# The scales of layer 2's norm, and its transposes, given out one step later than the statistics they need

## Chip, cores and metric

One core of a Trainium2 chip runs the whole program. The metric is the time on the device, in microseconds. The kernel before took 2642.23 us (median of three runs, 2640.15 to 2648.64); its profiled execution has a span of 2645.6 us.

## What is computed

Sixteen graphs of 1024 nodes with 256 features each go through four layers of graph network. Each layer normalises its input, applies relu, and adds its result to the stream `x`:

```python
h = jnp.maximum(_layernorm(x, axis=-1), 0.0)
x = x + _L2_gnn_ref(h, adj, L2_gnn_W_msg, L2_gnn_W_upd, L2_gnn_bias)
```

Layers 0, 1 and 3 are attention over the adjacency matrix (layer 3 with four heads and a norm of its own). Layer 2, whose norm the change is about, has no attention: it averages over the neighbours.

```python
h = jnp.einsum('bnf,fu->bnu', x, W_msg)
msg_sum = jnp.einsum('bij,biu->bju', a, h)
deg = jnp.sum(a, axis=1)
messages = jnp.where(deg[..., None] > 0, msg_sum / jnp.maximum(deg, 1.0)[..., None], 0.0)
out = jnp.einsum('bnf,fu->bnu', x, W_upd) + messages + bias
return jax.nn.relu(out)
```

## The kernel before

**Tiles.** A graph's stream `xs` lies in SBUF as eight tiles of 128 nodes x 256 features. Each layer has three steps: the norm with a transposition of its result into `ht` (features on partitions); a projection of the eight tiles (`project`, L678); and the product with the attention weights or the adjacency matrix (L749, L805, L868 and L874, L930). At the end of the products of layers 0 to 2, for i = 0 to 7, `residual` (from L719) adds the result to tile i of `xs`, and the statistics for the next layer's norm are taken there.

**The norm.** The class `Norm` works on pairs of tiles, g = 0 to 3. `pair` gets the sums of two tiles from `residual`, makes `shift`, the negative mean, on VectorE (L638), and lets ScalarE square the shifted tiles and sum them (L643, output `unread`). After every second pair, `stds` calls `inv_std`: GpSimd scales the four variances (L592) and raises them to the power -1/2 (L593), which gives `rs`. For layers 0, 1 and 3 the transposed values are only shifted, `hn = relu(x - mean)`, and the factor `rs` is applied after the projection. So their `hn` doesn't wait for the power. `shifted` makes two `hn` on ScalarE (L659), and `flip` transposes the two `hn` that are waiting (four transposes on TensorE, L672) and copies the result to `ht` (L673). `flip` is called one step after `shifted`, when the next pair begins.

Layer 2 differs: its norm (built with `times`, the degrees of the nodes) multiplies by the standard factor and by the degree before the transposition. So it needs `rs` first. `stds` makes two products on VectorE (L621 and L622): `scales[0] = rs * degree`, `scales[1] = scales[0] * shifts`. Then both pairs, g - 1 and g, are given out on the spot: `shifted` for pair g - 1, `flip`, `shifted` for pair g. That happens twice in layer 1's product: at i = 3 for tiles 0 to 3 and at i = 7 for tiles 4 to 7.

**The order of the work.** Each layer is a generator, and `graph(b)` runs a graph's layers one after the other. Each `yield` gives a number, the time that the step is taken to last in units of its own; a loop at the end of `tile_simple_stack` always continues the generator whose time comes first, and starts a new graph every 120 units (`APART`). A graph lasts some 237 units, and a tail of its own (`tail`, L942 to L992) follows, so the end of layer 1 of one graph is traced between the end of layer 3 and the tail of the graph before it and the first norm and layer 0's projection of the graph after it. That gives the program order. From it a planner makes each engine's queue: among the instructions that it takes to be ready, by costs of its own, the one traced first goes next. So an instruction can be issued earlier than its place in the program when the engine would otherwise stand. `later(...)` pins an instruction behind everything already traced on its engine. The tail's last products on VectorE are pinned in this way (L979, L982, L984, L986, L990), and so are most DMAs on the SyncE queue.

**Buffers concerned.** `hn` has three buffers, the PSUM tiles of the transposes (`tr`) two, those of the projections (`mm`) two, `ht` two, `rs` six. They are shared by all graphs under way.

**Lines.** L589 to L673 are `inv_std` and `Norm`; L719 to L729 `residual`; L792 and L736 copy a projection out of PSUM in layers 1 and 0 (`hs`), L859 and L861 in layer 2 (`hi`, `rest`); L826 to L830 are the end of layer 1 (`shares`, `e`, `v`); L1002 to L1006 the loop over the layers.

Of the kernel before, what the change touches and what calls it, by code (L numbers as in the profile page):

```python
# [11 lines left out]
OP = mybir.AluOpType  # L12
# [409 lines left out]
def tile_simple_stack(  # L422
# [11 lines left out]
    nc = tc.nc  # L434
    B, N, D = x.shape
    NT = N // P
# [111 lines left out]
    class Mask:  # L548
# [4 lines left out]
        def __init__(self, b):  # L553
            self.b, self.next, self.raws = b, 0, []
            self.bytes = None
            for _ in range(self.AHEAD):
                self.load()
# [31 lines left out]
    def inv_std(var, n, scale, eps):  # L589

        rs = small.tile([P, NT * H], F32, tag="rstd", name="rs", bufs=6)
        nc.gpsimd.tensor_scalar(rs[:, :n], var, scale, eps, op0=OP.mult, op1=OP.add)  # L592
        nc.gpsimd.tensor_tensor(rs[:, :n], rs[:, :n], neg_half[:, :n], op=OP.pow)  # L593
        return rs

    def new_ht():
        return state.tile([P, DC, N], F32, tag="ht", name="ht", bufs=2)

    class Norm:
# [4 lines left out]


        def __init__(self, times=None):
            self.ht, self.rs, self.waiting, self.times = new_ht(), [], None, times
            if times is not None:
                self.shifts = small.tile([P, NT], F32, tag="shifts", name="shifts", bufs=2)
                self.scales = small.tile([P, 2, NT], F32, tag="scales", name="scales", bufs=2)  # L610
            self.mv = small.tile([P, NT, 2], F32, tag="mv", name="mv", bufs=4)
            self.mean, self.var = self.mv[:, :, 0], self.mv[:, :, 1]

        def stds(self, n, scale):

            k = len(self.rs)
            rs = inv_std(self.var[:, k : k + n], n, scale, 1e-5)
            self.rs += [rs[:, i : i + 1] for i in range(n)]
            if self.times is not None:
                part = slice(k, k + n)  # L620
                nc.vector.tensor_tensor(self.scales[:, 0, part], rs[:, :n], self.times[:, part], op=OP.mult)  # L621
                nc.vector.tensor_tensor(self.scales[:, 1, part], self.scales[:, 0, part], self.shifts[:, part], op=OP.mult)  # L622

        def pair(self, xs, g, sums=None):

            if self.times is None:
                self.flip()
                shift = small.tile([P, 2], F32, tag="shift", name="shift")
            else:
                shift = self.shifts[:, 2 * g : 2 * g + 2]  # L630
            if sums is None:
                for k in range(2 * g, 2 * g + 2):
                    st = small.tile([P, 6], F32, tag="bn", name="st")
                    nc.vector.bn_stats(st, xs[:, k, :])
                    nc.vector.bn_aggr(self.mv[:, k, :], st)
                nc.vector.tensor_scalar(shift, self.mean[:, 2 * g : 2 * g + 2], -1.0, None, op0=OP.mult)
            else:
                nc.vector.tensor_scalar(shift, sums, -1.0 / D, None, op0=OP.mult)  # L638
            if self.times is None:
                self.shifted(xs, g, [(1.0, shift[:, k : k + 1]) for k in range(2)])  # L640
            if sums is not None:
                for k in range(2):
                    nc.scalar.activation(  # L643
                        unread, xs[:, 2 * g + k, :], AF.Square, bias=shift[:, k : k + 1], accum_out=self.var[:, 2 * g + k : 2 * g + k + 1]
                    )
            if sums is None and g == NT // 2 - 1:
                self.stds(NT, 1.0)
            elif sums is not None and g % 2:
                self.stds(NT // 2, 1.0 / D)
                if self.times is not None:  # L650
                    for gg in (g - 1, g):
                        self.flip()
                        self.shifted(xs, gg, [[self.scales[:, k, n : n + 1] for k in range(2)] for n in (2 * gg, 2 * gg + 1)])

        def shifted(self, xs, g, by):
            hns = []
# [62 lines left out]
    def residual(xs, i, v, after, e=None):  # L719

        x = xs[:, i, :]
        if i % 2 == 0:
            after.flip()
            after.sums = small.tile([P, 2], F32, tag="sums", name="sums")
        if e is not None:
            nc.vector.scalar_tensor_tensor(x, e, 1.0, x, op0=OP.min, op1=OP.add)  # L726
        nc.vector.scalar_tensor_tensor(x, v, 0.0, x, op0=OP.max, op1=OP.add, accum_out=after.sums[:, i % 2 : i % 2 + 1])  # L727
        if i % 2:
            after.pair(xs, i // 2, after.sums)  # L729


    def layer0(b, xs, m, norm, after):
# [40 lines left out]
        for i in range(NT):  # L773
            if i < EARLY:
                ps = early[i]
            else:
                ps = at_ps.tile([P, HALF], F32, tag="at", name="ps_o0")
                for j in range(NT):
                    product(ps, i, j)
            e = work.tile([P, D], F32, tag="e", name="e")  # L780
            nc.scalar.activation(e, ps[:, :D], AF.Exp)  # L781
            v = work.tile([P, D], F32, tag="v", name="v")
            nc.scalar.copy(v, ps[:, :D])
            residual(xs, i, v, after, e)
            yield 3.9


    def layer1(b, xs, mask, norm, after):
# [28 lines left out]
        for i in range(NT):  # L817
            if i < EARLY:
                ps = early[i]
            else:  # L820
                ps = at_ps.tile([P, HALF], F32, tag="at", name="ps_o1")
                for j in range(NT):
                    product(ps, i, j)
            k = b * NT + i
            z = shares[:, k : k + 1]
            nc.vector.reciprocal(z, ps[:, D : D + 1])  # L826
            e = work.tile([P, D], F32, tag="e", name="e")
            nc.scalar.activation(e, ps[:, :D], AF.Exp, scale=z)
            v = work.tile([P, D], F32, tag="v", name="v")
            nc.scalar.activation(v, ps[:, :D], AF.Copy, scale=z)  # L830
            residual(xs, i, v, after, e)
            yield 3.74


    def degrees(b):

        t = small.tile([P, NT], F32, tag="deg", name="deg", bufs=2)
        halves = squares[:, b * NT * NHALF : (b + 1) * NT * NHALF].rearrange("p (n g) -> p n g", g=NHALF)
        nc.vector.tensor_tensor(t, halves[:, :, 0], halves[:, :, 1], op=OP.add)
        return t  # L840
# [48 lines left out]
    def layer3(b, xs, mask, norm, res):  # L889
# [5 lines left out]
        for n in range(NT):  # L895
            ps = project(norm, wx[3], n, W3)
            nc.scalar.activation(hs[:, n, :], ps[:, :W3], AF.Copy, scale=norm.rs[n])
            if n % 2:
                pair = slice(n - 1, n + 1)
                nc.scalar.activation(hbv[:, pair, :, HO], terms[:, pair, H:], AF.Exp, scale=S3)  # L900
                t = hbv[:, pair, :, :HO]
                hv = hs[:, pair, :D].rearrange("p t (h e) -> p t h e", e=HO)
                bias = rows["bias3"].rearrange("p (h e) -> p h e", e=HO).unsqueeze(1).to_broadcast([P, 2, H, HO])
                nc.vector.tensor_tensor(t, hv, bias, op=OP.add)
                nc.vector.tensor_tensor(t, t, hbv[:, pair, :, HO:].to_broadcast([P, 2, H, HO]), op=OP.mult)
            yield 1.15
# [87 lines left out]
    def graph(b):  # L994
        xs = loaded.pop(b)
        m = masks.pop(b)
        norm = Norm()
        for g in range(NT // 2):
            norm.pair(xs, g)
            m.step()  # L1000
            yield 2.66
        for layer, inputs in ((layer0, (m,)), (layer1, (m.bytes,)), (layer2, ())):  # L1002
            yield 2.36
            norm.flip()
            after = Norm(degrees(b) if layer is layer1 else None)
            yield from layer(b, xs, *inputs, norm, after)  # L1006
            norm = after
        yield 1.44
        norm.flip()
        res = state.tile([P, NT, H, HW], F32, tag="res", name="res", bufs=1)  # L1010
        hs = yield from layer3(b, xs, m.bytes, norm, res)
        return tail(b, xs, hs, res)
# [22 lines left out]
    weights01(0, w0, w0_t, a0, (0, 1), wait=False)  # L1035
    next(loads_0)
    queue = [(32, 0, more())] + [(b * APART, b, graph(b)) for b in range(B)] + [(b * APART - 80, b, loads(b)) for b in range(1, B)]
    while queue:
        queue.sort(key=lambda g: g[:2])
        at, b, g = queue.pop(0)  # L1040
# [86 lines left out]
```

## Time and profile before

| | of the span of 2645.6 us |
|---|---|
| TensorE matmuls | 2470.5 us, 93% |
| TensorE weight loads | 2096.2 us, 79% |
| VectorE | 1969.1 us, 74% |
| ScalarE | 1449.8 us, 55% |
| GpSimd | 378.7 us, 14% |
| `hn` with scales (L659) | 128 x 592 ns |
| `scales` (L621, L622) | 64 x 0.16 us |
| transposes (L672) | 1024 x 273 ns |
| power (L593), four elements a partition, POOL free | 1.01 us |

The profile names engines PE (TensorE matmul), PEld (weight load, which overlaps PE), DVE (VectorE), ACT (ScalarE), POOL (GpSimd). A line of its timeline gives the start in microseconds from the span's start, the length, the engine, the source line, the operation, what is written and read, the shape, and in brackets the idle time of the engine just before and what ended it. In the answers for a tile, "its engine sat idle before it" lists the idle time before instructions that touch the tile, and "who waited for it" the idle time of others, each in microseconds in total and number of times. In steady state the trace repeats itself with every graph, some 158 us apart.

### The profile page before, as it was taken

The numbers are of one execution on the slowest core, as the hardware profiler recorded it, in microseconds if no ns is written. First come the engines' busy times: TensorE is split into PE (matmuls) and PEld (weight loads), VectorE is DVE, ScalarE is ACT, GpSimd is POOL, SyncE is SP. The second block draws the span as 40 slices with busy tenths as digits, with TensorE's granted clock in tenths as the row PEclk, the third lists the DMA queues.
The fourth block names the chain that finished last, engine by engine and source line by source line (L and its number), as shares of the span: only waits on it lengthen the run. The fifth ranks groups of instructions, "written<-read, shape, count | busy, mean of one in ns | idle before, by whom it ended". The sixth has DMA issues, their size and how long they took to land.

```text
span 2645.6 us, 62817 instructions
## 1 busy us (share of the span) xinstructions
PE 2470.5 (93%) x26194; PEld 2096.2 (79%) x26194; DVE 1969.1 (74%) x3813; ACT 1449.8 (55%) x4065; POOL 378.7 (14%) x390
## 2 busy tenths in 40 slices
PE   5899999999999999999999999999999999999985
PEld 4688787887878878787887878878787887878864
DVE  4357777787777877778787777877778787777858
ACT  4564755637555374654737556374754737556350
POOL 1010111102111020111102111020111102111011
PEclk7899999999999999999999999999999999999997
DMA  4431241414215142241414215141241414214021
GB/s 152 115 81 57 91 111 58 124 58 129 72 54 152 58 117 70 66 135 57 124 54 132 69 57 152 61 123 60 81 121 58 124 54 132 69 57 124 26 64 35
DMA packets 146073, 233.75 MB, mean 88 GB/s; under 512 B 9393, under 2 KB 94513, under 8 KB 145777
## 3 DMA queue, kind: packets, MB, share of 16 engines
q1 hardware_dynamic: 74608, 145.73, 17.3%
q0 software_dynamic: 71168, 83.89, 13.0%
q8 instruction: 208, 3.41, 0.5%
q14 instruction: 89, 0.72, 0.1%
HBM read 212.35 MB, written 17.24 MB: 87 GB/s over the span
## 4 chain that ended last, share of the span: by engine, by line
PE 60%; DMA 14%; ACT 10%; DVE 9%; issue 5%; POOL 2%; SPq 0%; DVEq 0%; ACTq 0%; POOLq 0%
PE ps_o L749 14%; PE ps_proj L678 14%; PE ps_o L930 10%; PE ps_o L805 8%; PE ps_o L874 6%; DMA raw<-in_adj_t 5%; PE pt_h L672 4%; DMA adj<-in_adj 4%; DVE p L920 3%; PE ps_o L868 3%; DMA row<-d_row 2%; ACT mask L575 2%; ACT hs L810 2%; ACT unread L643 2%; ACT hn L659 1%
## 5 line engine op out<-in xcount | busy, mean ns | idle before, releaser
L920 DVE SCALAR_TENSOR_TENSOR p<-row,q,mask 128x1024 f32<-128x1024 f32 x512 | 633.5, 1279 | 66.1 <-PE ps_o L930 53.2
L930 PEld LDWEIGHTS ps_o<-hb,p 128*64 128x64 f32 x16384 | 503.9, 138 | 99.9 <-issue 47.5
L930 PE MATMUL ps_o<-hb,p 128*64 128x65 f32 x16384 | 543.1, 224 | 19.8 <-ACT res L938 10.3
L805 PE MATMUL ps_o<-hs,p 128*128 128x257 f32 x2048 | 510.7, 392 | 31.0 <-DVE p L812 17.2
L678 PE MATMUL ps_proj<-wx,ht 128*128 128x258 f32 (+2 forms) x2048 | 515.7, 390 | 3.3 <-ACT hs L736 1.1
L749 PE MATMUL ps_o<-hs,p 128*128 128x256 f32 x2048 | 492.2, 385 | 13.6 <-ACT hs L763 13.3
L805 PEld LDWEIGHTS ps_o<-hs,p 128*128 128x128 f32 x2048 | 370.1, 191 | 96.1 <-ACT v L830 24.5
L749 PEld LDWEIGHTS ps_o<-hs,p 128*128 128x128 f32 x2048 | 380.7, 192 | 65.0 <-ACT hs L763 16.5
L678 PEld LDWEIGHTS ps_proj<-wx,ht 128*128 128x128 f32 x2048 | 361.9, 190 | 80.4 <-ACT rest L861 11.6
L726 DVE SCALAR_TENSOR_TENSOR xs<-e,xs 128x256 f32<-128x256 f32 x256 | 108.4, 424 | 261.0 <-ACT e L781 168.9
L592 POOL TENSOR_SCALAR rs<-mv 128x4 f32<-128x4 f32 (+1 forms) x112 | 44.3, 395 | 1583.2 <-ACT unread L643 1568.0
L659 ACT ACTIVATE hn<-xs,shift 128x256 f32<-128x256 f32 x384 | 177.1, 502 | 126.9 <-DVE shift L638 126.6
L593 POOL TENSOR_TENSOR rs<-rs,neg_half 128x4 f32<-128x4 f32 (+2 forms) x144 | 242.8, 1689 | 10.7
L672 PE MATMUL pt_h<-ident,hn 128*128 128x128 f32 x1024 | 181.1, 284 | 41.8 <-ACT hn L659 40.5
L874 PE MATMUL ps_o<-hi,adj 128*128 128x258 f32 x1024 | 202.9, 322 | 15.9 <-DMA adj<-in_adj 14.7
L938 ACT ACTIVATE res<-ps_o 128x260 f32<-128x260 f32 x128 | 44.4, 380 | 310.9 <-PE ps_o L930 310.9
L575 ACT ACTIVATE mask<-raw 128x512 uint8<-128x512 int32 x256 | 160.2, 627 | 76.5 <-DMA raw<-in_adj_t 75.8
L672 PEld LDWEIGHTS pt_h<-ident,hn 128*128 128x128 f32 x1024 | 121.3, 141 | 102.0 <-ACT hn L659 78.2
L874 PEld LDWEIGHTS ps_o<-hi,adj 128*128 128x128 f32 x1024 | 151.6, 190 | 33.3 <-DMA adj<-in_adj 20.3
L727 DVE SCALAR_TENSOR_TENSOR xs<-v,xs 128x256 f32<-128x256 f32 x384 | 161.2, 423 | 19.6 <-ACT v L830 1.0
L759 DVE SCALAR_TENSOR_TENSOR p<-row,q 128x1024 f32<-128x1024 f32 x128 | 160.2, 1272 | 20.2 <-DMA row<-d_row 20.2
L874 PE MATMUL ps_o<-lo,adj 128*128 128x258 f32 x1024 | 163.7, 293 | 0.0
(108 smaller groups left out, 2902.5 us busy)
## 6 DMA issues: line engine op xcount, KB each, us to landing
raw<-in_adj_t SPq DMA_DIRECT2D x256, 256.0 KB
adj<-in_adj POOLq DMA_DIRECT2D x64, 1024.0 KB, 6.0
row<-d_row SPq DMA_DIRECT2D x112, 512.0 KB
xs<-in_x POOLq DMA_DIRECT2D x32, 512.0 KB, 5.5
out<-xs SPq DMA_DIRECT2D x32, 512.0 KB
wx<-in_w SPq DMA_DIRECT2D x3, 256.0 KB
d_row<-e_row SPq DMA_DIRECT2D x48, 4.0 KB
wts<-in_w_t SPq DMA_DIRECT2D x2, 256.0 KB
```

What stands on the lines that cost most here:

```text
L575: nc.scalar.activation(self.bytes[:, n, g * HALF : (g + 1) * HALF], raw, AF.Square, accum_out=squares[:, k : k + 1])
L593: nc.gpsimd.tensor_tensor(rs[:, :n], rs[:, :n], neg_half[:, :n], op=OP.pow)
L659: nc.scalar.activation(hn, xs[:, 2 * g + k, :], AF.Relu, scale=scale, bias=bias)
L672: nc.tensor.transpose(pt[:, c, k * P : (k + 1) * P], hn[:, c * P : (c + 1) * P], ident)
L678: nc.tensor.matmul(ps[:, :width], norm.ht[:, c, n * P : (n + 1) * P], w[:, c, :width], start=(c == 0), stop=(c == DC - 1))
L727: nc.vector.scalar_tensor_tensor(x, v, 0.0, x, op0=OP.max, op1=OP.add, accum_out=after.sums[:, i % 2 : i % 2 + 1])
L749: m = nc.tensor.matmul(ps[:, :D], ps_[j][:, i * P : (i + 1) * P], hs[:, j, :D], start=(j == 0), stop=(j == NT - 1))
L759: nc.vector.scalar_tensor_tensor(p, row_a, q[:, j : j + 1], row_b, op0=OP.mult, op1=OP.max)
L805: nc.tensor.matmul(ps[:, : D + 1], ps_[j][:, i * P : (i + 1) * P], hs[:, j, : D + 1], start=(j == 0), stop=(j == NT - 1))
L874: nc.tensor.matmul(ps[:, : D + 2], adj_n[g][:, i, jj : jj + P], h[:, i, : D + 2], start=False, stop=(h is lo and i == NT - 1), skip_group_ ...
L920: nc.vector.scalar_tensor_tensor(p, row, q[:, jj, h : h + 1], mask[:, jj, :], op0=OP.max, op1=OP.mult)
L930: nc.tensor.matmul(pss[g][part, k * HW : (k + 1) * HW], ps_[t][:, i * P : (i + 1) * P][:, part], hbv[:, j + t, h, :], start=(j == 0 and t ...
```

## The change

The statistics stay where they are. `pair` notes after every second pair that a part of layer 2's norm is due, and the scales, the relu and the transposes of that part are given out by a new function, `settle`. It is called by `residual` before every odd tile, so for tiles 0 to 3 at i = 5 rather than at i = 3, and before the next layer begins, so for tiles 4 to 7 after layer 1's last step, two yields (3.74 and 2.36 units) later in the program. It is meant to keep the engines' queues from standing before instructions whose statistics are still under way. For the other norms `due` is None and `settle` does nothing. The arithmetic is the same.

```diff
@@ class Norm
         def __init__(self, times=None):
-            self.ht, self.rs, self.waiting, self.times = new_ht(), [], None, times
+            self.ht, self.rs, self.power, self.waiting, self.times, self.due = new_ht(), [], [], None, times, None
...
             self.rs += [rs[:, i : i + 1] for i in range(n)]
-            if self.times is not None:
-                part = slice(k, k + n)
-                nc.vector.tensor_tensor(self.scales[:, 0, part], rs[:, :n], self.times[:, part], op=OP.mult)
-                nc.vector.tensor_tensor(self.scales[:, 1, part], self.scales[:, 0, part], self.shifts[:, part], op=OP.mult)
+            self.power.append(rs[:, :n])
...
             elif sums is not None and g % 2:
                 self.stds(NT // 2, 1.0 / D)
-                if self.times is not None:
-                    for gg in (g - 1, g):
-                        self.flip()
-                        self.shifted(xs, gg, [[self.scales[:, k, n : n + 1] for k in range(2)] for n in (2 * gg, 2 * gg + 1)])
+                self.due = None if self.times is None else (xs, g)
+
+        def settle(self):
+
+            if self.due is None:
+                return
+            (xs, g), self.due = self.due, None
+            part = slice(2 * g - 2, 2 * g + 2)
+            k = (g // 2) * (NT // 2)
+            rs = self.power[g // 2]
+            nc.vector.tensor_tensor(self.scales[:, 0, part], rs, self.times[:, part], op=OP.mult)
+            nc.vector.tensor_tensor(self.scales[:, 1, part], self.scales[:, 0, part], self.shifts[:, part], op=OP.mult)
+            for gg in (g - 1, g):
+                self.flip()
+                self.shifted(xs, gg, [[self.scales[:, k, n : n + 1] for k in range(2)] for n in (2 * gg, 2 * gg + 1)])
@@ residual
-        if i % 2 == 0:
+        if i % 2:
+            after.settle()
+        else:
             after.flip()
             after.sums = small.tile([P, 2], F32, tag="sums", name="sums")
@@ graph
             yield 2.36
+            norm.settle()
             norm.flip()
```

## The prediction, made before the changed kernel had run

> **What bounds the kernel now.** I read the page first: the busy time of each engine and its 40 slices.
>
> ```profile
> PE 2470.5 (93%) x26194; PEld 2096.2 (79%) x26194; DVE 1969.1 (74%) x3813; ACT 1449.8 (55%) x4065; POOL 378.7 (14%) x390
> PE   5899999999999999999999999999999999999985
> PEclk7899999999999999999999999999999999999997
> ```
>
> TensorE is busy from the third slice to the third from the end at nearly full clock; no other engine comes near. The table by stretches of one graph's period in the middle of the run agrees (columns: length, then busy time of PE, PEld, DVE, ACT, POOL, then clock and DMA):
>
> ```profile
> 1404.00:1424.00 20.00, 18.13 (x87) 13.51 (x85) 8.43 (x29) 17.44 (x46) 11.32 (x10) 1.00 0.01 4
> 1404.00:1562.00 158.00, 153.22 (x1638) 129.82 (x1636) 123.47 (x238) 91.28 (x258) 24.43 (x25) 1.00 0.32 92
> ```
>
> PE stands idle for 158.00 - 153.22 = 4.8 us of a period, so what a change can save at most is the part of these 4.8 us that it touches. The 20 us from 1404 on, the end of layer 1, have 1.9 us of it and ACT at 87% beside it. Who ends the idle time there I took from the view of the tile `scales`, the one the diff moves:
>
> ```profile
>   POOL rs L593: 73.7, 32
>   DVE scales L622: 34.4, 32
> who waited for it (us, times):
>   PEld pt_h L672: 48.5, 50
>   ACT hn L659: 34.4, 32
>   PE pt_h L672: 30.3, 32
> ```
>
> Twice a graph, 32 times in all, VectorE stops at L621 for POOL's power (2.3 us each), ACT behind it (1.1 us), PE behind that (30.3 / 32 = 0.95 us). The timeline of the second stop of a graph, on DVE and then on ACT and PE (start, length, instruction, idle time before it):
>
> ```profile
> 1420.18 0.17 DVE L638 TENSOR_SCALAR shifts<-sums 128x2 f32<-128x2 f32 x1
> 1423.59 0.16 DVE L621 TENSOR_TENSOR scales<-rs,deg 128x4 f32<-128x4 f32 x1 [3.24 <-POOL rs L593]
> 1423.79 0.16 DVE L622 TENSOR_TENSOR scales<-scales,shifts 128x4 f32<-128x4 f32 x1
> 1423.87 1.22 DVE L979 TENSOR_TENSOR res<-res,row_gamma 128x1024 f32<-128x1024 f32 x1
> 1425.00 1.22 DVE L982 TENSOR_TENSOR res<-res,row_gamma 128x1024 f32<-128x1024 f32 x1
> ...
> 1423.98 0.60 ACT L659 ACTIVATE hn<-xs,scales 128x256 f32<-128x256 f32 x1 [1.44 <-DVE scales L622]
> 1424.49 0.46 ACT L859 ACTIVATE hi<-ps_proj,z 128x256 fp32r<-128x256 f32 x1
> ...
> 1418.12 5.18 PE L678 MATMUL ps_proj<-wx,ht 128*128 128x258 f32 x22
> 1424.63 0.88 PE L672 MATMUL pt_h<-ident,hn 128*128 128x128 f32 x6 [1.33 <-ACT hn L659]
> 1425.35 1.03 PE L678 MATMUL ps_proj<-wx,ht 128*128 128x258 f32 x4
> ```
>
> DVE stands still from 1420.35 to 1423.59 with a 1.22 us product of the other graph's tail (L979) behind it; PE has 22 projection matmuls done and the next four queued behind the transposes. The same list at the first stop (from 1404.7 on) has 1.46 us on DVE, 0.66 on ACT, 0.57 on PE. Event by event the PE waits of the 16 second stops sum to 20.2 us (mostly 1.29), those of the 16 first stops to 10.1 us (mostly 0.56, the first graph's 1.65).
>
> **What the Trainium skill says.** Perfetto Trace Analysis, section Tensor Engine Instruction: ACT, DVE and GPSIMD are strict FIFO and PE can only pull weight loads ahead. So one early-issued L621 holds all that follows; the trace agrees, L979 with its inputs long written starts right after L622. The same section says that a matmul's end is a model; so PE idle by matmuls (30.3 us) and by weight loads (48.5 us) bracket the true wait, and I use the smaller. GPSIMD Engine Reference, section 2.1: each POOL instruction goes through a software dispatch on eight cores, a price that doesn't shrink with the tile. The trace agrees: four elements a partition take 1.29 us for the two instructions of `inv_std` when POOL is free, and neither is touched by the diff.
>
> **The change part by part.** No instruction is added or removed: 32 times two DVE products (0.16 us each), 128 `hn` (0.59 us), 256 transposes and their copies stay. What moves is their place in the program, and with it the order that the planner gives each queue. `self.power` and `self.due` are Python, no work: nothing.
>
> *Second stop* (tiles 4 to 7, from i = 7). In the yields' units, counted from the graph's start, i = 7 of layer 1 is traced at 130.9 and `settle` now at 137.0 (3.74 + 2.36 later). The older graph, 120 ahead, traces its tail in between: L979 at 132.2, L982 at 133.7, L984 at 135.3, L986 at 136.8. These are pinned with `later`, each behind what its engine was given last; so before, L979 is pinned behind L622 and pays its wait, and after, it is pinned behind the shift L638. By the rows above its inputs are there. DVE then does up to four products at 1.14 us apart, 4 x 1.14 = 4.6 us from 1420.35, to 1424.9, in the 3.24 us in which it stands now. The power is ready at 1423.56, so L621 finds it done, at 1423.6 (two or three products ahead) to 1424.9 (four). DVE's wait goes. On ACT, `hi` and `rest` of layer 2's first tile (0.46 + 0.47 us) and the younger graph's `hs` (0.48) can go into the 1.44 us. On PE the projections L678 that stand behind the transposes, 1.03 us for four and 1.14 and 1.78 us for the next, go ahead; with ACT free to empty their PSUM tiles they fill 1.3 us. Value: 20.2 us less PE idle. Its cost: the chain hn, transposes, copy of `ht` (1423.98 to 1428.96 now) ends up to 1.3 us later; layer 2's tiles 0 to 3 need only the first half of `ht`, which is there, so I put the delay at nothing on PE, upper bound 1.3 us a graph.
>
> *First stop* (tiles 0 to 3, from i = 3). `settle` is traced at i = 5, 123.4 instead of 116.0. In front of L621 in DVE's queue only L727 of i = 4 (0.42 + 0.08 us) is added by priority, and it sits between L621 and L622 now; an idle queue may still take L621 as soon as the planner thinks that `rs` is there. So L621 probably still waits, but L622 comes 0.27 us sooner, at 1407.45: 16 x 0.27 = 4.3 us of PE's 10.1. Bounds: nothing and all 10.1. Queued behind the waiting L621 would then be L622 and the tail's L972, and for them wait the four `hn` and POOL's second `rs`.
>
> *New places.* The moved transposes still wait for `hn` as every other flip's do: those 192 flips cost PE 40.5 - 30.3 = 10.2 us in all, 0.053 each. For the 64 moved ones I charge 64 x 0.053 = 3.4 us.
>
> Sum: 20.2 + 4.3 - 3.4 = 21.1 us. 2642.2 - 21.1 = 2621.
>
> **The rivals.** (a) Both stops vanish, if L805, `e` and `v` of i = 5 fill the first one too: 30.3 - 3.4 = 26.9, time 2615. For it: PE has at 1408 to 1414 transposes, L868 and L678 to choose from. Against it: ACT is idle at 1407.3 and would take `hn` at once. (b) The planner puts L621 where it was, because it is ready by the planner's costs and DVE has nothing else: the order stays nearly as it is, 0 to 4 us, time 2640. For it: DVE is 42% busy in the stretch; tail work such as L958 and L961 is run ahead of its place already. Against it: L979 has stood right behind L622 in 15 of 16 graphs, which the pin explains. (c) Slower: the chain to `ht` starts 1.3 us later and nothing fills PE. Then the wait of 1.29 us becomes 2.6: 16 x 1.3 = 21 us more, 2663; half filled, 2653. For it: ACT has 87% there, three `hn` buffers are shared with the younger graph's norm, whose own pairs are traced at 120 to 128, so that the first stop's `hn` now fall among them. Against it: in the stretch PE always has projections of two graphs.
>
> **How the numbers follow.** Main case 0.55, (a) 0.12, (b) 0.13, (c) 0.20. Faster by over 0.3% (below 2634.3) is the main case and (a), 0.67; within 0.3% is (b), 0.13; slower 0.20. The range: below, all of the PE wait and some of the weight-load wait, 30.3 + a third of the other 18.2 = 36, 2606; above, (c) a little over half filled, 2656. What is left out is the worst half of (c) and a tail of gains over the bound, under 0.2.
>
> **What would show it.** In the changed profile: DVE's wait of `scales` for POOL (73.7 us) falls below 30; L979 starts right after L638 of i = 7; PE's wait for `hn` from `scales` falls from 30.3 to about 10; the idle PE time of a period falls by 1.3 us, the busy time stays. Wrong would be: PE waiting elsewhere for as much (L678 for `ht`, L805 for `v`, L874 for `hi`), L621 still next after L638, or a period with another order on PE that idles in layer 3 or 0, which this reasoning doesn't touch.

## The result, and the profile after

The changed kernel took 2633.36 us (median of four runs, 2629.24 to 2633.68) against 2642.64 us before in the same comparison: a ratio of 0.9958, 95% interval 0.9939 to 0.9977. That is 11 us less by the ratio, faster as forecast and inside the range, and about half of the 21 us forecast. The profiled runs lie farther apart (2645.6 and 2627.3 us) than the medians; single sums below are of these two executions, so they show where time went, not how much of it.

From the page of the kernel after, the busy time of each engine:

```profile
PE 2463.8 (94%) x26194; PEld 2095.5 (80%) x26194; DVE 1963.3 (75%) x3813; ACT 1446.5 (55%) x4065; POOL 387.7 (15%) x390
```

The instructions are the same in number, as they should be. PE stands idle for 2627.3 - 2463.8 = 163.5 us instead of 175.1, 11.6 less. By weight loads it is 531.8 instead of 549.4, 17.6 less, which is nearly the whole difference of the spans, 18.3. The idle time of the weight loads, which I had only used as the upper bracket, is the view that adds up here.

The view of the tile `scales` after (idle time before and behind, us and times):

```profile
  POOL rs L593: 37.8, 32
  DVE scales L658: 15.7, 17
who waited for it (us, times):
  PEld pt_h L680: 51.1, 50
  PE pt_h L680: 33.4, 32
  ACT hn L667: 15.7, 17
```

VectorE's wait for POOL has halved (73.7 to 37.8 us), and so has ScalarE's for VectorE (34.4 to 15.7). PE's wait for the scaled `hn` has not fallen: 33.4 us against 30.3, by weight loads 51.1 against 48.5. What fell is another wait. In the list of all waits (who waited for whom, us, times, longest), before and after:

```profile
PEld ps_o L805 <- ACT v L830: 24.5, 32, 2.2
...
PEld ps_proj L678 <- ACT hs L736: 10.2, 35, 1.3
```

```profile
PEld ps_proj L686 <- ACT hs L746: 13.9, 50, 1.3
...
PEld ps_o L815 <- ACT v L840: 9.0, 15, 1.3
```

Layer 1's products (L805, L815 after) waited 24.5 us for `v` to leave their PSUM tile, and now 9.0: 15.5 us less, the largest change among TensorE's waits. The order on ScalarE suggests a reason: before, it made `v` of i = 4 at 1404.62 and `e` of i = 5 only at 1413.23, with eight `hn` and three `ht` copies between; now `e` and `v` of i = 5 precede the four scaled `hn`. But the waits themselves say otherwise. Of the 24.5 us, 18.2 were for `v` of i = 4 and 3.6 for `v` of i = 5, and `v` of i = 4 stands in front of the scaled `hn` in both kernels. The products of i = 6 wait for it, since they write into its PSUM tile (16 matmuls for each i). Before, on PE and ACT:

```profile
1393.91 10.67 PE L805 MATMUL ps_o<-hs,p 128*128 128x257 f32 x48
1404.62 0.46 ACT L830 ACTIVATE v<-ps_o,shares 128x256 f32<-128x256 f32 x1
1405.13 2.87 PE L805 MATMUL ps_o<-hs,p 128*128 128x257 f32 x12 [0.56 <-ACT v L830]
```

After:

```profile
1390.64 0.60 PE L680 MATMUL pt_h<-ident,hn 128*128 128x128 f32 x4
1391.08 7.20 PE L815 MATMUL ps_o<-hs,p 128*128 128x257 f32 x32
1394.03 0.46 ACT L840 ACTIVATE v<-ps_o,shares 128x256 f32<-128x256 f32 x1
```

Before, the products of i = 3, 4 and 5 run in a row, and those of i = 6 have to wait. After, four transposes of the younger graph's first norm stand between the products of i = 4 and i = 5, and when those of i = 6 begin, `v` is there. (Also, `v` of i = 4 ends 4.0 us after the products of i = 4 instead of 4.4, the middle values of twelve graphs.) The younger graph's `hn` that these transposes need now run ahead of the four scaled ones, the first three from 1380.64 us on; before, they all came behind. They share three buffers with the scaled `hn`, which are now traced later; that this is why they run ahead is a reading of the program and was not tested.

The second stop of a graph after, from the timeline on DVE, then ACT and PE:

```profile
1408.24 0.17 DVE L635 TENSOR_SCALAR shifts<-sums 128x2 f32<-128x2 f32 x1
1408.32 1.22 DVE L989 TENSOR_TENSOR res<-res,row_gamma 128x1024 f32<-128x1024 f32 x1
1409.46 1.22 DVE L992 TENSOR_TENSOR res<-res,row_gamma 128x1024 f32<-128x1024 f32 x1
1410.59 1.22 DVE L994 TENSOR_TENSOR res<-res,rs 128x1024 f32<-128x1024 f32 x1
1412.71 0.16 DVE L657 TENSOR_TENSOR scales<-rs,deg 128x4 f32<-128x4 f32 x1 [0.90 <-POOL rs L593]
1412.81 1.20 DVE L996 TENSOR_TENSOR res<-res,row_beta 128x1024 f32<-128x1024 f32 x1
...
1413.93 0.15 DVE L658 TENSOR_TENSOR scales<-scales,shifts 128x4 f32<-128x4 f32 x1
...
1414.12 2.07 ACT L667 ACTIVATE hn<-xs,scales 128x256 f32<-128x256 f32 x4 [0.91 <-DVE scales L658]
...
1414.78 0.44 PE L680 MATMUL pt_h<-ident,hn 128*128 128x128 f32 x2 [0.81 <-ACT hn L667]
```

The tail's products L989, L992 and L994 (L979, L982, L984 before) stand right behind the shift, as forecast, and fill what was a wait of 3.24 us. But the planner issues L657 in front of the fourth, L996, and there it still waits 0.90 us; L996 then gets between L657 and L658, and `hn` starts 1.44 us after the power instead of 0.43. PE's wait falls from 1.33 only to 0.81. From the shift to the first `hn` it is now 5.88 us, and was 3.80: PE waits less although `hn` comes later, because its projections last longer: they end 5.7 us after the shift, before 3.1.

That L657 waits at all has a cause on GpSimd. The power of this stop before and after:

```profile
1422.55 1.01 POOL L593 TENSOR_TENSOR rs<-rs,neg_half 128x4 f32<-128x4 f32 x1
```

```profile
1410.82 1.86 POOL L593 TENSOR_TENSOR rs<-rs,neg_half 128x4 f32<-128x4 f32 x1
```

Its scaling (L592) went from 0.20 to 0.74 us as well, so the two take 2.69 us, from the start of the one to the end of the other, instead of 1.29. Before, VectorE stood still meanwhile; after, it runs the tail's products. The 14 stops between the first graph and the last show the same to 0.01 us. With 1.29 us, by an estimate from these rows, the power would have been there at 1411.28, before the third product ended at 1411.81.

The first stop before, on DVE, ACT and PE:

```profile
1407.29 0.16 DVE L621 TENSOR_TENSOR scales<-rs,deg 128x4 f32<-128x4 f32 x1 [1.46 <-POOL rs L593]
...
1407.91 1.58 ACT L659 ACTIVATE hn<-xs,scales 128x256 f32<-128x256 f32 x3 [0.66 <-DVE scales L622]
...
1408.56 0.93 PE L672 MATMUL pt_h<-ident,hn 128*128 128x128 f32 x4 [0.57 <-ACT hn L659]
```

After, in the same way:

```profile
1395.85 0.16 DVE L657 TENSOR_TENSOR scales<-rs,deg 128x4 f32<-128x4 f32 x1 [0.90 <-POOL rs L593]
1395.93 1.22 DVE L971 SCALAR_TENSOR_TENSOR res<-m,res 128x1024 f32<-128x1024 f32 x1
...
1397.49 0.14 DVE L658 TENSOR_TENSOR scales<-scales,shifts 128x4 f32<-128x4 f32 x1
...
1397.18 1.06 ACT L974 ACTIVATE sq<-res 128x1024 f32<-128x1024 f32 x1 [0.86 <-DVE res L971]
1398.15 0.46 ACT L838 ACTIVATE e<-ps_o,shares 128x256 f32<-128x256 f32 x1
1398.51 0.47 ACT L840 ACTIVATE v<-ps_o,shares 128x256 f32<-128x256 f32 x1
1398.86 0.59 ACT L667 ACTIVATE hn<-xs,scales 128x256 f32<-128x256 f32 x1
...
1399.51 0.88 PE L680 MATMUL pt_h<-ident,hn 128*128 128x128 f32 x6 [1.24 <-ACT hn L667]
```

ScalarE no longer waits in front of `hn`, but PE waits 1.24 us for it instead of 0.57. The chain goes around: POOL holds L657 for 0.90 us, L657 holds the tail's L971, L971 holds the tail's square on ScalarE for 0.86 us, and `e`, `v` and `hn` stand behind the square. Added event by event, PE's waits at the first stops are 19.4 us (10.1 before), at the second 13.9 us (20.2 before).

### The profile page after: what moved, and what is told of

It is laid out like the page before. It is cut to its first block, busy times and chain, and to the rows that moved or that the text cites. A ratio compares the mean times of both kernels' runs of the same rounds, so it can differ in the third digit from the quotient of the medians.

```text
span 2627.3 us, 62786 instructions
## 1 busy us (share of the span) xinstructions
PE 2463.8 (94%) x26194; PEld 2095.5 (80%) x26194; DVE 1963.3 (75%) x3813; ACT 1446.5 (55%) x4065; POOL 387.7 (15%) x390
## 4 chain that ended last, share of the span: by engine, by line
PE 55%; ACT 16%; DMA 11%; DVE 9%; issue 6%; POOL 2%; SPq 0%; DVEq 0%; POOLq 0%; ACTq 0%
PE ps_o L759 16%; PE ps_proj L686 12%; PE ps_o L940 11%; PE ps_o L884 6%; PE ps_o L815 6%; ACT hn L667 4%; DMA adj<-in_adj 4%; DMA raw<-in_adj_t 3%; DVE p L930 3%; PE pt_h L680 3%; ACT unread L640 2%; PE ps_o L878 2%; ACT ht L681 2%; POOL rs L593 2%; ACT mask L575 2%
## 5 line engine op out<-in xcount | busy, mean ns | idle before, releaser
L815 PE MATMUL ps_o<-hs,p 128*128 128x257 f32 x2048 | 506.7, 391 | 19.7 <-DVE p L822 16.1
L686 PE MATMUL ps_proj<-wx,ht 128*128 128x258 f32 (+2 forms) x2048 | 513.1, 391 | 5.8 <-ACT hs L746 4.4
L815 PEld LDWEIGHTS ps_o<-hs,p 128*128 128x128 f32 x2048 | 369.5, 190 | 79.3 <-DVE p L822 10.5
L686 PEld LDWEIGHTS ps_proj<-wx,ht 128*128 128x128 f32 x2048 | 363.3, 190 | 83.4 <-ACT hs L746 13.9
L592 POOL TENSOR_SCALAR rs<-mv 128x4 f32<-128x4 f32 (+1 forms) x112 | 38.5, 344 | 1569.6 <-ACT unread L640 1554.6
L593 POOL TENSOR_TENSOR rs<-rs,neg_half 128x4 f32<-128x4 f32 (+2 forms) x144 | 257.2, 1789 | 10.7
L769 DVE SCALAR_TENSOR_TENSOR p<-row,q 128x1024 f32<-128x1024 f32 x128 | 159.8, 1269 | 17.7 <-DMA row<-d_row 17.6
```

The source lines that it names most:

```text
L686: nc.tensor.matmul(ps[:, :width], norm.ht[:, c, n * P : (n + 1) * P], w[:, c, :width], start=(c == 0), stop=(c == DC - 1))
L769: nc.vector.scalar_tensor_tensor(p, row_a, q[:, j : j + 1], row_b, op0=OP.mult, op1=OP.max)
L815: nc.tensor.matmul(ps[:, : D + 1], ps_[j][:, i * P : (i + 1) * P], hs[:, j, : D + 1], start=(j == 0), stop=(j == NT - 1))
```

## The experiments

Two theories came out of this. A: the gain comes from the first stop, where `e` and `v` of i = 5 were freed (before the waits were told apart by i, as above), and the wait that is left comes from the planner, which still issues the products of the scales as soon as it takes `rs` to be ready. B: the gain comes from the second stop, as the prediction had it. All ratios are against the kernel before, run on the same chip; its median there was 2651 to 2656 us, so ratios, not times, are compared.

**The two halves alone.** Two lines more in `pair` give the other half out on the spot, as before. First the first half of the change alone, then the second:

```diff
                 self.due = None if self.times is None else (xs, g)
+                if g == NT // 2 - 1:
+                    self.settle()
```

> Only the first half of the change: tiles 0 to 3 are given out at i = 5, tiles 4 to 7 on the spot at i = 7 as before. Theory A (read from the changed trace: the gain comes from the first stop, where e and v of i = 5 no longer stand on ScalarE behind four hn, so that the products L805 get their PSUM tile): 2632 to 2637, PE's wait of L805 for v falls from 13.8 us to under 5, and the wait for the scaled hn at the first stop doubles from 10 to about 20 us. Theory B (the gain comes from the second stop, as the prediction had it): 2640 to 2645.

```diff
                 self.due = None if self.times is None else (xs, g)
+                if g < NT // 2 - 1:
+                    self.settle()
```

> Only the second half of the change: tiles 0 to 3 on the spot at i = 3 as before, tiles 4 to 7 at the start of layer 2. Theory A: DVE's wait at the second stop falls from 3.1 to about 0.9 us, but PE's only from 1.29 to about 0.8, because a tail product of 1.2 us is issued between the two products of the scales; 16 x 0.4 = 6 us at most, so 2636 to 2641. Theory B: most of the gain of the whole change, 2631 to 2635.

The first half took 0.9978 (0.9968 to 0.9987), the second 1.0043 (1.0026 to 1.0061): 0.4% slower than before. B falls. Of A, the first half came as forecast, at the weak end (2632 to 2637 us are 0.996 to 0.998 of 2642.6), and so did its two waits (L805's for `v` 4.5 us on PE, the scaled `hn` 19.1 at the first stops); for the second half A forecast a small gain too (0.997 to 0.999), and missed. The second half did what it was meant to do at its own place: by events, DVE's wait at the second stop fell from 49.1 to 16.4 us and PE's from 20.2 to 8.3. Yet the run was slower. ScalarE's timeline and the list of waits of this kernel show part of where it went:

```profile
1428.88 2.07 ACT L669 ACTIVATE hn<-xs,scales 128x256 f32<-128x256 f32 x4 [1.20 <-DVE scales L660]
```

```profile
PEld ps_proj L688 <- ACT rest L873: 20.0, 78, 0.5
...
PEld ps_o L886 <- ACT hi L871: 8.2, 18, 0.7
```

The weight loads' waits of the projections for `rest` and of layer 2's products for `hi` are 20.0 and 8.2 us, against 11.6 and 2.6 before. The four `hn` stand in a row, where before `hi` and `rest` of the first tile came between. The halves also don't add up: -0.2% and +0.4% alone, -0.4% together, so by the means the second half is worth -0.2% beside the first and costs 0.4% without it. The intervals of the first half and of the whole overlap, so that only the end of the loss is shown, not the gain.

**The tail product between the two products of the scales.** With `moved = shift x degree` multiplied beforehand, the second product needs only `rs`; the line that uses it:

```diff
...
-            nc.vector.tensor_tensor(self.scales[:, 1, part], self.scales[:, 0, part], self.shifts[:, part], op=OP.mult)
+            nc.vector.tensor_tensor(self.scales[:, 1, part], rs, self.moved[:, part], op=OP.mult)
```

> The whole change, with the second product of the scales made from rs and from shift x degree, which is multiplied beforehand (32 x 2 small products more, 0.16 us each), so that it doesn't wait for the first and stands right behind it. If the tail product between the two is what keeps PE's wait at 13.9 us at the second stop and lengthens it at the first, hn starts about 1.2 us sooner after rs at both, the second PE wait falls to under 5 us, and the time to 2620 to 2628. If PE's wait is set by the order on PE and ACT alone, it stays at 2630 to 2636.

The ratio was 0.9966 (0.9953 to 0.9979), no better than the change itself. The two products stood back to back, and PE's wait at the second stop fell from 13.9 to 8.0 us, not below 5 as expected, and at the first from 19.4 to 13.9. So the product between was a part of the wait, and taking 11 us of PE's wait at these two places away gave no time.

**Pinned.** The planner is kept from issuing the first product ahead of its place:

```diff
-            nc.vector.tensor_tensor(self.scales[:, 0, part], rs, self.times[:, part], op=OP.mult)
+            later(nc.vector.tensor_tensor(self.scales[:, 0, part], rs, self.times[:, part], op=OP.mult))
```

> The whole change, with the first product of the scales pinned behind everything traced before it on VectorE, so that the planner can't issue it earlier than its place. If the issue ahead of its place is what kept the wait, DVE's wait of the scales for POOL falls from 38 us to under 5, PE's wait for the scaled hn from 33 to under 20, and the time to 2620 to 2629. If the later hn only move the wait to other places (L686 for ht, L815 for v), the time stays at 2630 to 2638.

0.9890 (0.9870 to 0.9910), more than twice the gain of the change and more than was expected. DVE's wait missed its forecast: 14.6 us, not under 5. From its view of `scales`, and from DVE's timeline at the second stop:

```profile
  POOL rs L593: 14.6, 15
  DVE scales L658: 4.5, 16
who waited for it (us, times):
  PEld pt_h L680: 20.0, 37
  PE pt_h L680: 7.3, 19
```

```profile
1401.39 1.22 DVE L996 TENSOR_TENSOR res<-res,row_beta 128x1024 f32<-128x1024 f32 x1
1402.53 0.15 DVE L657 TENSOR_TENSOR scales<-rs,deg 128x4 f32<-128x4 f32 x1
1402.72 0.16 DVE L658 TENSOR_TENSOR scales<-scales,shifts 128x4 f32<-128x4 f32 x1
```

This is the queue that the prediction had drawn for the change: four tail products, then the scales without a wait. The power takes 2.69 us here too, but it has ended 0.31 us before L657 begins. PE's wait for the scaled `hn` is 7.3 us. Something is given back: the projections' wait for `hs` (L686) rose to 23.7 us by weight loads, from 13.9 with the change.

**Which stop the pin helps.** The pin at one stop only: in the first half alone (condition g == 1, and the second half given out on the spot), and in the whole change, which is shown:

```diff
-            nc.vector.tensor_tensor(self.scales[:, 0, part], rs, self.times[:, part], op=OP.mult)
+            scaled = nc.vector.tensor_tensor(self.scales[:, 0, part], rs, self.times[:, part], op=OP.mult)
+            if g > 1:
+                later(scaled)
```

> First half of the change alone, with its first product pinned to its place; tiles 4 to 7 on the spot at i = 7 as before. If the first stop carries the gain of the pinned kernel (1.1% in all), because there L621 of before holds L971, the tail's square on ScalarE, e and v and then hn, this has 0.990 to 0.995 of the time before, against 0.998 for the same half without the pin. If the gain is in the second stop: 0.996 to 0.999.

> The whole change, with the pin at the second stop only. If the first stop carries the gain, this stays near the change itself, 0.994 to 0.997; if the second does, 0.989 to 0.992. DVE's wait at the second stop is 0, at the first 0.9 to 1.5 us as with the change.

The first half alone with its pin: 0.9941 (0.9922 to 0.9961), against 0.9978 without it. The whole change with the pin at the second stop only: 0.9952 (0.9935 to 0.9970), no different from the change. There DVE's wait at the second stop was 2.9 us and PE's 2.2, instead of 16.4 and 13.9, and again time didn't follow. Its list of waits shows why:

```profile
PEld ps_proj L688 <- ACT hs L748: 23.8, 50, 1.3
...
PE ps_proj L688 <- ACT hs L748: 14.1, 15, 1.1
```

With the change these were 13.9 and 4.4 us: of the 11.7 us that PE no longer waits for `hn`, 9.7 came back at the projections, which wait for `hs` to leave their PSUM tile. The rise in the pinned kernel is this one. The pin matters at the first stop, where the product holds L971, the square, `e` and `v`. There PE's wait fell from 19.1 to 4.9 us in the first half alone and from 19.4 to 5.0 between this run and the pinned one, and time followed, by 0.4% and 0.6%.

**Later still.** Tiles 0 to 3 at i = 7, without a pin, then with both pins:

```diff
-        if i % 2:
+        if i % 4 == 3:
             after.settle()
-        else:
+        if i % 2 == 0:
```

> The whole change, with tiles 0 to 3 given out at i = 7 instead of i = 5 (no pin). If only the distance from the statistics counts, the planner still issues the products as soon as it takes rs to be ready, so DVE's wait at the first stop stays at 0.5 to 1.5 us; but e and v of i = 5 and 6 and their reciprocals come ahead, so PE's wait at the first stop falls from 19 to under 12 us: 0.990 to 0.995. If the four hn then crowd ScalarE at the end of layer 1, 0.996 to 1.003.

> Tiles 0 to 3 at i = 7 (0.9901 without a pin) and both first products pinned to their places (0.9890 at i = 5). If the two do the same thing, bringing e and v of i = 5 and 6 ahead of the four hn: 0.988 to 0.992. If they add up: 0.980 to 0.986. If the eight hn crowd the end of layer 1 together with the younger graph's: 0.992 to 1.000.

0.9901 (0.9875 to 0.9927), and 0.9875 (0.9855 to 0.9895). The first of them had PE's waits for the scaled `hn` at the first stop at 9.6 us in all, instead of 19.4. Both reach what the pin reaches at i = 5: the intervals overlap, and the two gains don't add up, though the second mean lies just below the range given for that.

**Without the power.** POOL is left out of layer 2's norm, at the old and at the new places; the factor is then `var x scale + eps`, so these kernels compute layer 2 of something else. One VectorE instruction stands in place of the two on POOL, the rest is the same. The new instruction:

```diff
...
+                nc.vector.tensor_scalar(rs[:, :n], self.var[:, k : k + n], scale, 1e-5, op0=OP.mult, op1=OP.add)
```

> The kernel before, at its old places, with POOL left out of layer 2's norm: the factor is var x scale + eps, made on VectorE, without the power, so layer 2's input is scaled differently. It measures what the round trip over POOL costs where the scales stood: if the planner's cost for the power (1.0 to 1.3 us on POOL, which it seems to take for less) is the root of both stops, the DVE wait before the scales falls from 74 us to under 20, PE's wait for the scaled hn from 30 to under 12, and the time to 0.988 to 0.994. If the planner's orders are short on PE and ACT for another reason, 0.996 to 1.000.

> The changed kernel with POOL and the power left out of layer 2's norm (the factor is var x scale + eps, made on VectorE, so layer 2's input is scaled differently). At the old places the same took 0.995 of the time before. If the wait for POOL is what the change leaves on the table, this gains on the change (0.9958) by 5 us or more: 0.988 to 0.994. If ScalarE's order around layer 2's projections is what limits, as the rise of the waits for hi and rest in the run without the power at the old places says, 0.994 to 0.999.

At the old places 0.9950 (0.9936 to 0.9965), between the two forecasts; at the new ones 0.9861 (0.9839 to 0.9883), more than forecast. The view of `scales` and the list of waits of the first of them, at the old places:

```profile
who waited for it (us, times):
...
  PEld pt_h L676: 8.8, 33
...
  PE pt_h L676: 0.3, 2
```

```profile
PEld ps_proj L682 <- ACT rest L865: 22.1, 75, 0.6
PEld ps_o L809 <- ACT v L834: 21.4, 19, 2.3
PEld ps_o L878 <- ACT hi L863: 11.0, 21, 1.7
```

This run tells most. PE's wait for the scaled `hn` is gone, 0.3 us instead of 30.3, by weight loads 8.8 instead of 48.5, and the time fell by 0.5%, some 13 us. The rest came up at the projections' wait for `rest` (11.6 to 22.1) and at `hi` (2.6 to 11.0), while the wait for `v` stayed at 21.4. So 30 us of PE's wait at the stops were worth 13 us of time. At the new places, without POOL, the kernel reaches what the pin reaches with POOL. So the round trip over POOL is what the change left, and the pin hides most or all of it (the intervals overlap). The tail's own powers on POOL have no part in this: in the profiles before and after, and in the one without the power at the new places, no engine waits for them.

**The four `hn` in a row.** The second half of the change alone again, with the `hn` of tiles 6 and 7 traced after layer 2's second projection and their transposes after the fourth; and the same spreading in the whole pinned change; the part in layer 2:

```diff
...
             nc.vector.tensor_tensor(lo[:, n, :D], rest, hi[:, n, :D].bitcast(F32), op=OP.subtract)
+            if n == 1:
+                norm.rest()
+            elif n == 3:
+                norm.flip()
```

> The second half of the change alone (1.0043), with the two hn of tiles 6 and 7 traced after layer 2's second projection and their transposes after the fourth, so that ScalarE has hn, hn, hi, rest, hn, hn instead of four hn in a row. If the row of four hn ahead of hi and rest is what makes the second half slower than before (PSUM tiles of the projections are emptied 1 us later), 0.995 to 1.001. If it is the later end of ht, which is later still here, 1.004 to 1.010.

> The whole change, both first products pinned, and the hn of tiles 6 and 7 spread as in the run before this one. If the row of four hn costs the pinned kernel its new wait of L686 for hs (41 us by weight loads, 25 before), that wait falls below 30 us and the time to 0.981 to 0.987; otherwise as the pinned kernel, 0.988 to 0.991, or above it if the later ht holds layer 2.

The second half spread took 0.9972 (0.9961 to 0.9983) instead of 1.0043. The wait that was to fall did:

```profile
PEld ps_proj L697 <- ACT rest L882: 7.5, 34, 0.3
PEld ps_o L899 <- ACT hi L880: 5.3, 21, 1.8
```

That is 7.5 instead of 20.0 for `rest` and 5.3 instead of 8.2 for `hi`. The order of these `hn` decides whether the second half gains or loses, though the layer's `ht` is complete later (13.7 us after the second stop's shift instead of 9.3, the middle values of twelve graphs); how much of it is the row itself stays open, since other waits of that execution moved as well. In the whole pinned change the spreading brought 0.9877 (0.9852 to 0.9903), no different from the pin alone: there its wait for `hs` fell to 7.4 us from 23.7 (the 41 and 25 us in the expectation do not stand in the lists of waits, which have 23.7 and 13.9), and ScalarE's wait for the transposes rose to 34.6 us from 9.9.

## Why the prediction was right or wrong

The direction and the range held, the size by luck: the sum was 21 us, the gain 11, and most of that sum came from a place where it was not won. By its own steps:

- *PE bounds the kernel, and 4.8 us of a period are the most to be had.* PE stayed the bound. But the idle time by matmuls was a poor measure of what can be saved: between the profiled runs it fell by 11.6 us and the weight loads' idle by 17.6, with a difference of the spans of 18.3. The second half alone had less matmul idle at the two stops together than before (18.4 us against 30.3) and took longer.
- *L979 pinned behind L622, free after.* Right: it stands behind the shift now, and three tail products go ahead.
- *DVE's wait at the second stop goes.* Two thirds of it went, 49.1 to 16.4 us. I let two to four products go ahead; the planner let three, and yet L657 waits 0.90 us, with L996 behind it. I had the power ready when it was before, at 1.29 us for its two instructions, because the diff doesn't touch them; beside the tail's products they take 2.69. Nor are the 1.29 us a fixed price, as I had read the dispatch: the power of sixteen elements a partition takes 2.90 us, that of four 1.01. And I had not seen that a product could get between the two of the scales, though I had noted just this of L727 at the first stop.
- *20.2 us less PE idle at the second stop.* This is the step that failed. It was 6.3 us by events, 13.9 us being left; and, as the second half alone and the pin at the second stop only show, PE's wait at this place is mostly not time. In the stretch ScalarE is 87% busy before and 90% after (18.09 of 20 us; both stretches end 1.45 us after the second power began), and the projections wait for it to empty their PSUM tiles: a wait that is taken off the transposes comes back at `rest`, `hi` or `hs`. The cost that I had put at nothing is here too: counted from the shift, the first `hn` comes some 2 us later and `ht` is complete 1.8 us later, more than the bound of 1.3.
- *4.3 us at the first stop.* Wrong sign at the line itself: 10.1 us became 19.4. And yet the first half alone gains 0.22%, and the wait that fell there is another, of layer 1's products for `v` of i = 4 (15.5 us less in the whole change, 13.8 in the first half alone). The kernels with tiles 0 to 3 at the new place, ten of them, have transposes of another norm between the products of i = 4 and of i = 6, and PE waits at most 0.52 us before the latter; the other three and the kernel before have none there and wait 0.88 to 0.96 (middle values of twelve graphs). I had no term for this. Rival (a), "if L805, `e` and `v` of i = 5 fill the first one too", was right that `e` and `v` go ahead; but neither stop vanished; at the first, the square in front of them waited for L971.
- *3.4 us for the moved transposes.* This took it that the moved transposes would wait as every other flip's do, 0.053 us each. After the other two terms it left some 9 us of wait; it was 33.4, 0.52 for each of the 64 flips.
- *The rivals.* (b), that the planner issues L621 where it takes it to be ready, is what happened in part: DVE's wait is still 37.8 us, and the pin, which forbids it, doubles the gain. (c), that the later chain costs layer 2 more than it brings, is what the second half does when it stands alone, 0.43%. The forecast came out in the middle of its range because a gain that I hadn't counted (at `v`) stood in for one that didn't come.

Of the signs that it named, L979 behind the shift came; DVE's wait is 37.8 us and not below 30, PE's wait for the scaled `hn` 33.4 and not about 10, and PE's idle time fell by 0.7 us a graph and not by 1.3 (11.6 us over 16 graphs).

The sum that the runs put in its place: the first half brings -0.2%, the second +0.4% alone and -0.2% beside the first. Why the second half costs nothing beside the first, where it loses 0.4% alone, was not settled.

Perfetto Trace Analysis in the Trainium skill, section Tensor Engine Instruction, says that the end of a matmul is modelled. The runs agree with the caution that follows from it: busy PE time was 2463.8 us in one and 2470.5 us in the other with the same 26194 matmuls, while the weight loads' was 2095.5 and 2096.2.

## What to carry to other kernels

A wait of the bounding engine is worth its time only if what it waits for was the last obstacle, as it mostly was at the first stop here and not at the second: before a sum of waits is taken for a gain, look which engine empties the PSUM tiles of the work behind it, and how busy that is in the stretch. Where a planner orders the queues, moving an instruction later in the program does not move it as far in the queue if the planner takes it to be ready; pinning it, or taking away the slow producer, is a different change and shows what the move was worth (here 0.4% by the move, 1.1% with the pin). Work that is moved into a wait can lengthen it: beside the tail's products, the power that was waited for took 2.69 us with its scaling instead of 1.29. A wait that falls should be traced to the very instruction that ended it, not to the nearest one of its line (`v` of i = 4, not of i = 5). And an instruction that waits should be followed through the queue behind it, engine by engine: the 0.9 us on VectorE reached PE by way of a tail product and a square that have nothing to do with the norm.

## What was not expected of the hardware

Four elements a partition take POOL 1.29 us for the two instructions of the power when it and VectorE are free, and 2.69 us while VectorE runs the tail's 128 x 1024 products; what in these products slows POOL the profile doesn't tell. The move with these 32 round trips taken out, and the move with the pin, which hides most of them, bring 1.4% and 1.1%, where the move alone brings 0.4%, in a kernel in which POOL is busy 15% of the time. And the idle time of the weight loads followed the span within 1 us in the runs before and after, when matmul idle did not: the same matmuls in another order had 6.7 us less of matmul busy time. Over all thirteen changed kernels, weight-load idle misses the difference of the spans by up to 7.6 us and matmul idle by up to 15.8; in two of the thirteen matmul idle is the nearer.
